# A second early row in every other block of a graph-attention kernel

## The chip, the cores and the metric

The kernel runs on one core of one Trainium2 chip. A core has five engines that each follow their own list of instructions: TensorE (PE in the profile), VectorE (DVE), ScalarE (ACT), GpSimd (POOL) and SyncE (SP), which here only issues DMAs. They meet at semaphores. Sixteen DMA engines move the data. The metric is the device time of one execution, in microseconds.

## The reference

There are N = 30000 nodes with 256 features and E = 510000 edges, sorted by their destination; every edge has one of 8 relations.

```python
x = x + gnn(layernorm(x), conv_weights, attn_l, attn_r, h_bias, src, dst, edge_type)
x = x + ffn(layernorm(x))

def gnn(...):                                   # 8 relations, 4 heads of 64
    feat_all = einsum('ni,rhid->rnhd', inputs, conv_weights)
    feat_src_e, feat_dst_e = feat_all[edge_type, edge_src], feat_all[edge_type, edge_dst]
    el = sum(feat_src_e * attn_l[edge_type], -1)
    er = sum(feat_dst_e * attn_r[edge_type], -1)
    e = leaky_relu(el + er, 0.2)
    alpha = softmax of e over the edges of one destination    # segment max, exp, segment sum
    return segment_sum(alpha * feat_src_e, edge_dst).reshape(N, 256) + h_bias
```

`ffn` is a shared three-layer perceptron plus four experts, each a three-layer perceptron, of which the two with the highest gate are weighed and added.

## The kernel before, in words

The work has two large stages.

**The features.** 235 tiles of 128 nodes are normalised, transposed and multiplied with the weights of all relations and heads (L305). Copies on ACT and DVE (L307, L309) put the products into buffers `fo`, and SyncE stores them (L319) to `feat` in DRAM: one row of 4 x 65 numbers (1040 bytes) for each node and relation, 64 features and the left score of each head. Beside these tiles run three generators, one step at a time in fixed places of the tile loop (`aside`): `edge_records` makes one record of each edge, `places` lays the edges out for attention, and `expert_weights` loads the experts' weights.

`places` cuts the edges into 252 blocks, twelve a batch. Each block has 128 partitions x 16 places (U = 16), each place one edge. It writes a record `rk` for each block to DRAM: the indices of the rows to gather (WI), the destinations (WD), marks (WA), penalties at the borders between destinations (WP), running minima of them (W1) and the one-hot relations (WT).

In each partition one of the 16 edges has the lowest row number. `places` swaps it into place 0 and keeps, in `mark`, where it came from. Because the features are computed in order of the rows, this early row can be fetched before the features end: `first_rows` gathers it on POOL by an indirect DMA into `fr` and SyncE stores four blocks together to `stage` in DRAM. This begins at tile 178 of 235 (`BT + 2`), at a rate of 252 gathers over the tiles that are left, and the gather may touch the first 176 tiles' rows only. A check of the indices leads to a second path of the kernel (`again`) if a row lies beyond.

**Attention.** 252 blocks and one last block of its own form. The loop runs over iterations t, each with six steps c, and the order on every engine is the order in which the code is written (`manual_schedule`). Stages of several blocks are in flight in one iteration:

- `load(t + 2)`: SyncE loads the record `rk` (L903), destinations `dr` (L921), right scores `erp` (L924), residual rows `xt` (L926). `rk` has five buffers.
- `gather(t + 1)`: SyncE loads the early rows from `stage` (L931); POOL issues 15 indirect gathers of one place each (L933) into `ft`, a ring of four blocks. A place of the ring is free when `sums` of the block four earlier is done with it.
- `flags(t + 1)` and `flags_across` spread the penalties (ACT L951 to L955, PE transposes L962, ACT copy L964).
- `dest_select`, `dest_expand` and `dest_pick` (L987 on PE, L998 and L1000 on DVE) give each edge its right score.
- `scores(t)` adds the two scores and takes the running maximum of each destination, forwards and backwards (scans L1032 and L1033, results `fb`). As the swap of `places` has moved one edge of each partition to place 0, `exchange` (L1018, L1020, L1022) swaps the scores to the edges' order before the scans, and `softmax` swaps them again after them.
- `turn_ends` (L1040, L1041), `across` (scans L1047 and L1048), `turn_back` (L1055, L1056) carry the maxima across partitions.
- `softmax` (L1062 to L1065) and `exps` (L1071, L1072) make the weights, `weigh` (L1079) multiplies the rows by them, `onehot` (ACT L1010, L1011) and `sums` (PE L1086) add them by destination into `po`, `finish` divides.
- `residual_sum` adds the input (L1117) and calls `Experts.stats`, the mean and variance for the second layer norm (L722, L723).

Every four blocks one group `Experts` is ready. Its 22 steps (`spread`, `scale` L734, `turn` with the copy L744, the layers L798 to L854, `last` with L857) are taken one in each step c. At the end of a group `last` issues four stores of output rows on SyncE (L1097), in the same queue as the loads.

The parts of `gather` and `exchange` that the change touches read:

```python
nc.sync.dma_start(s.ft[:, 0]..., stage[t * P:(t + 1) * P, :])
for u in range(1 if s.own else 0, s.u):
    nc.gpsimd.indirect_dma_start(out=s.ft[:, u]..., in_=feat[:, :], ...)
```

Of the kernel before, what the change touches and what calls it, by code (L numbers as in the profile page):

```python
# [10 lines left out]
F32 = mybir.dt.float32  # L11
# [10 lines left out]
P = 128  # L22
# [23 lines left out]
WI, WD, WA, WP, W1, WT, WR = 0, U, 2 * U, 3 * U, 4 * U + 1, 6 * U + 3, 6 * U + 3 + U * 4  # L46
# [7 lines left out]
def kernel(  # L54
# [47 lines left out]
    stage = dram.tile([NBLK * P, H * HW], F32, name="stage")  # L102
# [71 lines left out]
    NPEN = 3  # L174
    pens = []
    for i in range(NPEN + 1):
        f = wf.tile([P, H, U if i < NPEN else UL], F32, name=f"penf{i}")
        b = wf.tile([P, H, U if i < NPEN else UL], F32, name=f"penb{i}")
        nc.gpsimd.memset(f, -BIG)
        nc.gpsimd.memset(b, -BIG)  # L180
        pens.append((f, b))
    carry = []
    for i in range(2):
        cf = wf.tile([H, P + 1], F32, name=f"carf{i}")
        cb = wf.tile([H, P + 1], F32, name=f"carb{i}")
        nc.gpsimd.memset(cf, -BIG)
        nc.gpsimd.memset(cb, -BIG)
        carry.append((cf, cb))
# [33 lines left out]
    with ExitStack() as cx:  # L222
# [263 lines left out]
        BT = 3 * NT // 4  # L486
        count = {"ready": 0, "sent": 0}
        low = gp.tile([P, NBLK], I32, name="low")
        lowc = gp.tile([P, NBLK], I32, name="lowc")

        def places(cl):


            GB = 12
# [28 lines left out]
            yield  # L523
            done = None
            for k, (b0, n) in enumerate(batches):
# [4 lines left out]
                key = kp.tile([P, GB, U], F32, name="key", bufs=1)[:, :n]  # L530
                km = kp.tile([P, GB], F32, name="km", bufs=1)[:, :n]
                x = rc[:, :, :U, :3].rearrange("p b u f -> p b f u")
                mark = of[:, :, WA:WA + U]
                nc.vector.scalar_tensor_tensor(key, rc[:, :, :U, 0], float(U),
                                               iu[:, None, :].to_broadcast([P, n, U]), op0=ALU.mult, op1=ALU.add)
                nc.vector.tensor_reduce(km, key, AX.X, ALU.min)
                yield
                if done:
                    done()
                nc.vector.tensor_tensor(mark, key, km[:, :, None].to_broadcast([P, n, U]), op=ALU.is_equal)  # L540
                m3 = mark[:, :, None, :].to_broadcast([P, n, 3, U])
                t3 = kp.tile([P, GB, 3, U], F32, name="t3", bufs=1)[:, :n]
                nc.vector.tensor_mul(t3, x, m3)
                yield
                for f in range(3):
                    nc.vector.copy_predicated(x[:, :, f, 1:], o[:, :, WA + 1:WA + U],
                                              x[:, :, f, 0:1].to_broadcast([P, n, U - 1]))
                yield
                with nc.allow_low_precision(reason="integers below 2 ** 24"):
                    nc.vector.tensor_reduce(x[:, :, :, 0], t3, AX.X, ALU.add)  # L550
                yield
# [3 lines left out]
                nc.gpsimd.tensor_copy(low[:, b0:b0 + n], rc[:, :, 0, 0])  # L555
                nc.gpsimd.tensor_scalar_min(lowc[:, b0:b0 + n], rc[:, :, 0, 0], float(BT * P * R - 1))
                nc.gpsimd.tensor_copy(o[:, :, WI:WI + U], rc[:, :, :U, 0])
                count["ready"] = b0 + n
                pen = kp.tile([P, GB, UW], F32, name="penk")[:, :n]
                nc.vector.tensor_scalar_mul(pen, rc[:, :, :, 3], -BIG)  # L560
                yield
                nc.gpsimd.tensor_copy(of[:, :, WP:WP + UW], pen)
                d16 = kp.tile([P, GB, U], I16, name="d16k")[:, :n]
                nc.gpsimd.tensor_copy(d16, rc[:, :, :U, 1])
                a1 = kp.tile([P, GB, UW], F32, name="a1k")[:, :n]
                a2 = kp.tile([P, GB, UW], F32, name="a2k")[:, :n]
# [7 lines left out]
                nc.gpsimd.tensor_copy(of[:, :, W1 + UW:W1 + 2 * UW], a2)  # L574
                yield
# [7 lines left out]
                def done(o=o, d16=d16, b0=b0, n=n):  # L583
                    nc.sync.dma_start(rk_d[b0:b0 + n].rearrange("b p w -> p b w"), o)
                    nc.sync.dma_start(dk_d[b0 * CAP:(b0 + n) * CAP].rearrange("(b p u) -> p b u", p=P, u=U), d16)
            yield
# [3 lines left out]
            nc.vector.tensor_reduce(exc, low, AX.X, ALU.max)  # L590
# [9 lines left out]
            nc.vector.tensor_scalar(both[:, 0:1], both[:, 0:1], float(BT * P * R), None, op0=ALU.is_ge)  # L600
# [3 lines left out]
        def first_rows():  # L604

            n, kept = 4, []
            fp = cl.enter_context(tc.tile_pool(name="first", bufs=3))

            def keep(b0, m, fr):
                nc.sync.dma_start(stage[b0 * P:(b0 + m) * P, :].rearrange("(b p) f -> p b f", p=P), fr[:, :m])  # L610
            for b0 in range(0, NBLK, n):
                m = min(n, NBLK - b0)
                fr = fp.tile([P, n, H * HW], F32, name="fr")
                for b in range(m):
                    nc.gpsimd.indirect_dma_start(
                        out=fr[:, b], out_offset=None, in_=feat[0:BT * P * R, :],
                        in_offset=bass.IndirectOffsetOnAxis(ap=lowc[:, b0 + b:b0 + b + 1], axis=0))
                    if b == n // 2 and kept:
                        keep(*kept.pop())
                    count["sent"] += 1  # L620
                    yield
                kept.append((b0, m, fr))
            while kept:
                keep(*kept.pop(0))

        with tc.manual_schedule():
# [49 lines left out]
            for m in range(lead, NT - 1):  # L676
                for g in range(NG):
# [6 lines left out]
                    if m >= BT + 2:  # L684
                        fetched = min(fetched + 1.03 * NBLK / ((NT - BT - 2) * NG), 3)
                        while fetched >= 1 and count["sent"] < count["ready"]:
                            next(ahead)
                            fetched -= 1
# [13 lines left out]
    class Experts:  # L702
# [3 lines left out]
        def __init__(self, pool, ph, pc, x1, n, put):  # L706
            self.pool, self.ph, self.pc, self.x1, self.n, self.put = pool, ph, pc, x1, n, put
            self.w = n * M
            self.mv = pool.tile([P, T, 2], F32, name="c_mv", bufs=2)
# [10 lines left out]
        def stats(self, t):  # L720
            st = self.pool.tile([P, 6], F32, name="c_st")
            nc.vector.bn_stats(st[:M], self.x1[:M, t, :])  # L722
            nc.vector.bn_aggr(self.mv[:M, t, :], st[:M])  # L723

        def spread(self):
            self.rs = self.pool.tile([P, T], F32, name="c_rs")
            nc.scalar.activation(self.rs[:M, :self.n], self.mv[:M, :self.n, 1], AF.Sqrt, bias=eps[:M])

        def scale(self, j):
            if j == 0:  # L730
                nc.vector.reciprocal(self.rs[:M, :self.n], self.rs[:M, :self.n])
                self.xn = self.pool.tile([P, T, D], F32, name="c_xn")
            for t in range(j, min(j + 2, self.n)):
                nc.vector.tensor_scalar(self.xn[:M, t, :], self.x1[:M, t, :], self.mv[:M, t, 0:1],  # L734
                                        self.rs[:M, t:t + 1], op0=ALU.subtract, op1=ALU.mult)
# [126 lines left out]
    with ExitStack() as cx:  # L862
# [17 lines left out]
        flat = "p h u -> p (h u)"  # L880
        blk = {}

        class Block:


            def __init__(self, t):
# [7 lines left out]
                self.pens = pens[t % NPEN if t < NBLK else NPEN]  # L894

        def load(t):
# [3 lines left out]
            if s.own:  # L900
# [6 lines left out]
                s.mark, s.marki = rf[:, WA:WA + U], rk[:, WA:WA + U]  # L907
# [497 lines left out]
```

## Time and profile before

| | us |
|---|---|
| runs, median of 3 (lowest to highest) | 8389.48 (8380.45 to 8390.53) |
| profiled execution | 8380.65 |
| its span in the trace | 8379.0 |
| end of the features, about | 1746 |
| first gather of attention | 1750.45 |
| last exponentials, about | 8354 |

The profiled execution is one run. Its span is the time from the first to the last instruction of the trace, and 1.65 us lie around it. Busy time of an engine is the time in which it executes; idle time before an instruction is put down to what released it. "issue" stands for an engine that waited for nothing that the profile shows, and "remote" for a semaphore event whose sender it can't name. A row of the timeline gives start, duration, engine, line, operation, tile names as out<-in, sizes, and in brackets the idle time before it with its releaser. The windows table gives the busy time of each engine in a stretch of time, with the granted clock of PE, the share of the DMA engines that was busy, and the data rate.

### The profile page before, as it was taken

The page shows a single profiled execution, that of the slowest core. Times are in us where ns is not written, and L with a number is a line of the kernel's source. Part 1 is how long each engine was busy: PE and PEld are TensorE (multiplying, and loading weights), DVE is VectorE, ACT ScalarE, POOL GpSimd, SP SyncE. Part 2 cuts the span into 40 slices and gives each one's busy share as a digit, 9 for nine tenths or more (in the row PEclk, how much of TensorE's full clock was granted, in tenths as well). Part 3 has the DMA queues.
Part 4 walks back from the last instruction along what each step waited for, and adds up shares of the span by engine and source line. Part 5 has one row for each costly group of instructions (what it writes and reads, how often), then busy time and mean ns, then how long its engine had stood idle before and what let it go on. Part 6 is the DMA issues. An engine that isn't in the chain of part 4 may idle for free. (4 is left out here: it accounts for less than half of the span.)

```text
span 8379.0 us, 96556 instructions
## 1 busy us (share of the span) xinstructions
PE 6330.2 (76%) x25254; PEld 3986.0 (48%) x25255; DVE 5381.4 (64%) x13882; ACT 3416.7 (41%) x9511; POOL 4073.5 (49%) x4327
## 2 busy tenths in 40 slices
PE   9999999956666767777666667777666777777667
PEld 5555555534444444444444444444444444444444
DVE  5557774447666666666666666666666666666665
ACT  2222222224444444444444444444444444444444
POOL 1101114665555555555555555555555555555552
PEclk9999999978888888888888888888888888888888
DMA  6657778964444444444444444444444444444441
GB/s 226 229 177 238 224 243 303 341 197 123 116 117 117 118 116 119 119 121 119 117 120 117 119 116 118 118 123 118 118 116 117 118 119 118 116 119 117 115 118 55
DMA packets 761457, 1209.52 MB, mean 144 GB/s; under 512 B 241638, under 2 KB 599789, under 8 KB 730685
## 3 DMA queue, kind: packets, MB, share of 16 engines
q1 hardware_dynamic: 565453, 663.56, 24.8%
q0 software_dynamic: 194400, 539.40, 23.3%
q8 instruction: 206, 3.38, 0.2%
q14 instruction: 358, 2.93, 0.1%
q10 hardware_dynamic: 1040, 0.26, 0.0%
HBM read 818.57 MB, written 384.23 MB: 144 GB/s over the span
## 5 line engine op out<-in xcount | busy, mean ns | idle before, releaser
L933 POOL DMA_INDIRECT ft<-feat,rk x3798 | 3608.6, 950 | 2919.9 <-PE po L1086 956.0
L1086 PE MATMUL po<-ft,oh 128*128 128x260 f32 x8100 | 2305.4, 421 | 286.3 <-DVE ho L1107 149.5
L1086 PEld LDWEIGHTS po<-ft,oh 128*128 128x128 f32 x8100 | 1565.4, 208 | 569.7 <-issue 292.4
L305 PE MATMUL ps<-w,xT 128*128 128x448 f32 (+1 forms) x4700 | 1712.6, 519 | 14.3 <-DVE xT L294 8.6
L1079 DVE TENSOR_TENSOR ft<-ft,p 128x768 f32<-128x768 f32 x1518 | 1289.9, 850 | 394.8 <-issue 184.1
L1010 ACT ACTIVATE oh<-icol,rk 128x128 f32<-128x128 f32 x4032 | 1329.1, 389 | 66.4 <-remote 45.5
L305 PEld LDWEIGHTS ps<-w,xT 128*128 128x128 f32 x4700 | 877.3, 191 | 704.9 <-issue 613.5
L798 PE MATMUL ph<-xT,w 128*128 128x512 f32 (+1 forms) x512 | 372.1, 859 | 961.8 <-issue 888.7
L307 ACT COPY fo<-ps 128x448 f32<-128x448 f32 (+1 forms) x711 | 377.3, 533 | 1087.4 <-PE ps L305 912.4
L998 DVE TENSOR_TENSOR ere<-pe,rk 128x384 f32<-128x384 f32 x1008 | 553.3, 549 | 373.4 <-remote 247.9
L1011 ACT ACTIVATE oh<-oh 128x384 f32<-128x384 f32 x1518 | 740.2, 488 | 49.4
L987 PEld LDWEIGHTS <-ohT 128*128 128x128 bf16 x4050 | 393.9, 158 | 548.8 <-issue 438.1
L798 PEld LDWEIGHTS ph<-xT,w 128*128 128x128 f32 x512 | 112.3, 260 | 1112.1 <-issue 952.5
L744 ACT COPY xT<-ph 128x512 f32<-128x512 f32 (+1 forms) x128 | 73.1, 572 | 1325.3 <-remote 1299.9
L1000 DVE TENSOR_REDUCE e<-ere 128x16 f32<-128x384 f32 (+1 forms) x1012 | 561.5, 555 | 34.8
L987 PE MATMUL pe<-erp,ohT 128*128 128x96 bf16 x4050 | 442.3, 236 | 113.3 <-DVE ohT L970 73.5
L798 PE MATMUL ph<-xT,v 128*128 128x512 f32 (+1 forms) x1024 | 500.2, 613 | 2.3 <-ACT h L799 1.5
L1062 DVE TENSOR_TENSOR c<-t,rk 128x128 f32<-128x128 f32 x252 | 71.8, 285 | 618.9 <-remote 582.0
L1071 ACT ACTIVATE p<-e 128x64 f32<-128x64 f32 (+1 forms) x253 | 70.4, 278 | 844.9 <-DVE e L1022 741.8
L307 DVE COPY fo<-ps 128x448 f32<-128x448 f32 (+1 forms) x464 | 242.3, 528 | 221.9 <-PE ps L305 194.2
L1040 PE MATMUL t<-ident,fb 128*4 128x128 f32 x253 | 70.8, 280 | 383.6 <-DVE fb L1033 196.7
L851 PE MATMUL pf<-w,h 128*128 128x256 f32 x506 | 203.2, 491 | 189.1 <-ACT wT L844 85.1
(206 smaller groups left out, 7422.2 us busy)
## 6 DMA issues: line engine op xcount, KB each, us to landing
feat<-fo SPq DMA_DIRECT2D x234, 1040.0 KB
dr<-dk_d SPq DMA_DIRECT2D x252, 516.0 KB
ft<-feat,rk POOLq DMA_INDIRECT x3798
stage<-fr SPq DMA_DIRECT2D x63, 520.0 KB
ft<-stage SPq DMA_DIRECT2D x252, 130.0 KB
xt<-xb_d SPq DMA_DIRECT2D x253, 128.0 KB
out_dram<-og SPq DMA_DIRECT2D x253, 128.0 KB
xb_d<-xb SPq DMA_DIRECT2D x58, 512.0 KB
```

What stands on the lines that cost most here:

```text
L305: nc.tensor.matmul(ps, t["xT"][:, k, :], w[:, k, c0:c1], start=k == 0, stop=k == 1)
L307: eng(t["fo"][:, h0:h1, :HD], ps[:, :n].rearrange("p (a d) -> p a d", d=HD))
L798: nc.tensor.matmul(ps[:, :self.w], lhs, rhs, start=i == 0, stop=i == len(pairs) - 1)
L851: nc.tensor.matmul(pf[:M], self.h2[:, tok], w3, start=True, stop=False)
L933: nc.gpsimd.indirect_dma_start(out=s.ft[:, u].rearrange("p h d -> p (h d)"), out_offset=None, in_=feat[:, :], in_offset=bass.IndirectOffse ...
L987: nc.tensor.matmul(pe[:, u - u0].rearrange("p f r -> p (f r)"), s.ov[:, u, :], s.erp.rearrange("n h k r -> n (h k r)"), start=True, stop=True)
L998: nc.vector.tensor_mul(ere, s.pe[:, :u1 - u0], s.th[:, u0:u1, None, :].to_broadcast([P, u1 - u0, H * 3, R]))
L1000: nc.vector.tensor_reduce(s.e[:, :, u0:u1].rearrange("p h u -> p u h"), ere.rearrange("p u (h k) r -> p u h (k r)", h=H), AX.X, ALU.add)
L1010: nc.scalar.activation(s.oh[:, u, :], icol, AF.Abs, bias=s.nd[:, u:u + 1])
L1011: nc.scalar.activation(s.oh[:, u0:u1], s.oh[:, u0:u1], AF.Relu, bias=1.0, scale=-1.0)
L1079: nc.vector.tensor_mul(fc, fc, pc[:, :, None].to_broadcast([P, (u1 - u0) * H, HD]))
L1086: nc.tensor.matmul(s.po.rearrange("n h d -> n (h d)"), s.oh[:, u, :], s.ft[:, u].rearrange("p h d -> p (h d)"), start=u == 0, stop=u == s. ...
```

## The change

In even blocks the second place holds an early row as well. In the diff, `i` counts the early rows of a block.

- `places` makes a second exchange for every other block, over the places 1 to 15: the lowest row of these goes to place 1. The record holds two marks and grows from 163 to 194 words. A batch takes 11 steps and no longer 9.
- `first_rows` gathers 252 + 126 rows, three to a buffer and store. It starts at tile 156 (`FIRST`), at 1.02 x 378 gathers over the remaining 78 tiles. Each gather may touch the rows stored by then (`rows_there`) and no longer a fixed number of tiles.
- `gather` loads one or two early rows from `stages` and issues 15 or 14 indirect gathers. There are 3672 of them in place of 3798.
- `exchange` is called twice in `scores` and twice in `softmax`; the second call does nothing in odd blocks.
- `flags` makes one copy on ACT in place of four. What `flags_across` computed in each block is made in `places`, twelve blocks at once, written to `thr_d`, and loaded in `load` into `through`.
- `turn_ends` uses two accumulating matmuls, the second against a reversed identity (`turned`), so that both directions run in one scan of eight partitions in `across`, followed by a copy that turns the second half.
- `Experts.stats` and `Experts.scale` move from DVE to ACT: two passes with `accum_out` (Identity and Square) and a small one between them, and the scaling as an activation with scale and bias.

```diff
@@ first_rows, places @@
-        BT = 3 * NT // 4
+        NF = (NBLK, (NBLK + 1) // 2)
+        FIRST = NT * 2 // 3
+        RATE = 1.02 * sum(NF) / (NT - 1 - FIRST)
+        def rows_there(i, b0):
+            at = b0 - b0 % GB if i == 0 else NBLK + b0 - b0 % (GB // 2)
+            return min(NT - 2, int(FIRST + at / RATE) - 2) * P * R
...
+                for i in range(2):
+                    v = rc[:, ::i + 1, i:U]
+                    m, w = (n + i) // (i + 1), U - i
...
+                nc.tensor.transpose(ps[:, :P], a1[:, :, U - 1], ident)
+                nc.tensor.matmul(ps[:, P:], a2[:, :, 1], turned, start=True, stop=True)
+                thr = kp.tile([GB, 2 * P], F32, name="thr")[:n]
+                nc.scalar.copy(thr, ps)
...
-                    if m >= BT + 2:
-                        fetched = min(fetched + 1.03 * NBLK / ((NT - BT - 2) * NG), 3)
+                    if m >= FIRST:
+                        fetched = min(fetched + RATE / NG, 3)
@@ Experts @@
         def stats(self, t):
-            nc.vector.bn_stats(st[:M], self.x1[:M, t, :])
-            nc.vector.bn_aggr(self.mv[:M, t, :], st[:M])
+            nc.scalar.activation(sq[:M], self.x1[:M, t, :], AF.Identity, accum_out=st[:, 0])
+            nc.scalar.activation(st[:, 1], st[:, 0], AF.Identity, scale=-1.0 / D)
+            nc.scalar.activation(sq[:M], self.x1[:M, t, :], AF.Square, bias=st[:, 1], accum_out=st[:, 2])
...
-                nc.vector.tensor_scalar(self.xn[:M, t, :], self.x1[:M, t, :], self.mv[:M, t, 0:1],
-                                        self.rs[:M, t:t + 1], op0=ALU.subtract, op1=ALU.mult)
+                nc.scalar.activation(self.xn[:M, t, :], self.x1[:M, t, :], AF.Identity, bias=rs[:, 1, t:t + 1],
+                                     scale=rs[:, 0, t:t + 1])
@@ load, gather @@
+                self.early = 2 - t % 2 if self.own else 0
...
+                s.through = lp.tile([2 * H, P], F32, name="through", bufs=3)
+                nc.sync.dma_start(s.through, bass.AP(tensor=h.tensor, offset=h.offset, ap=[[P, 2], [0, H], [1, P]]))
...
-                nc.sync.dma_start(s.ft[:, 0].rearrange("p h d -> p (h d)"), stage[t * P:(t + 1) * P, :])
-            for u in range(1 if s.own else 0, s.u):
+            for i in range(s.early):
+                b = t >> i
+                f = b % NS * H * HW
+                nc.sync.dma_start(s.ft[:, i].rearrange("p h d -> p (h d)"), stages[i][b // NS, :, f:f + H * HW])
+            for u in range(s.early, s.u):
@@ flags, exchange, across @@
+            if s.own:
+                nc.scalar.copy(s.pens, s.pen[:, :, None, :].to_broadcast([P, 2, H, n]))
+                return
...
-            exchange(s, s.e)
+            exchange(s, s.e, 1)
+            exchange(s, s.e, 0)
...
-            nc.tensor.transpose(s.t1[:, 0, :], s.f[:, :, s.u - 1], ident)
-            nc.tensor.transpose(s.t1[:, 1, :], s.b[:, :, 0], ident)
+            s.t1 = turned_rows("t1", rows[:, :2 * H, s.u - 1], rows[:, 2 * H:4 * H, 0])
...
-            nc.vector.tensor_tensor_scan(cf[:, 1:], s.through[:, 0, :], s.t1[:, 0, :], -BIG, ALU.add, ALU.max)
-            nc.vector.tensor_tensor_scan(cb[:, P - 1::-1], s.through[:, 1, ::-1], s.t1[:, 1, ::-1], -BIG,
-                                         ALU.add, ALU.max)
+            nc.vector.tensor_tensor_scan(cf[:, 1:], s.through, s.t1, -BIG, ALU.add, ALU.max)
+            nc.vector.tensor_copy(cb, cf[:, P - 1::-1])
```

## The prediction

> **What bounds the kernel now.** I read four views, in this order. The page's busy shares first: no engine is full over the span, so the stages must be taken apart.
>
> ```profile
> PE 6330.2 (76%) x25254; PEld 3986.0 (48%) x25255; DVE 5381.4 (64%) x13882; ACT 3416.7 (41%) x9511; POOL 4073.5 (49%) x4327
> DMA  6657778964444444444444444444444444444441
> ```
>
> The DMA row has its peak (9 and 6) at the end of the features and stands at 4 for the whole attention. So, second, the windows table over the features (columns: window, PE, PEld, DVE, ACT, POOL busy, clock, DMA share, GB/s).
>
> ```profile
> 1200.00:1300.00 100.00, 100.00 (x302) 54.27 (x301) 62.22 (x171) 26.30 (x56) 15.09 (x18) 1.00 0.74 231
> 1400.00:1450.00 50.00, 50.00 (x152) 27.17 (x151) 19.97 (x66) 12.73 (x27) 34.65 (x34) 1.00 1.00 353
> ```
>
> PE is full in both: a tile takes 7.3 us and nothing else shows through. But in the second window, where the early rows are gathered beside the features, the DMA engines are full too, at 353 GB/s. The features have no DMA to spare there.
>
> Third, the waits.
>
> ```profile
> ACT xT L744 <- remote: 1299.9, 63, 22.3
> POOL ft L933 <- PE po L1086: 956.0, 427, 19.8
> DVE c L1062 <- remote: 582.0, 61, 20.3
> ```
>
> 63 times, once for each group of four blocks, ACT waits some 20 us for a PE result in PSUM ("remote": the profile names no sender). The starts of the exponentials (L1071) give the same rhythm: their intervals have medians 36.6, 22.4, 22.0 and 22.2 us, so four blocks take 103.0 us, of which about 14.5 are a stall. Fourth, the timeline across one stall, SyncE's queue and POOL, then who starts again:
>
> ```profile
> 4985.52 13.04 SPq L1097 DMA_DIRECT2D out_dram<-og  x4
> 4999.51 0.33 SPq L903 DMA_DIRECT2D rk<-rk_d  x1
> ...
> 4982.54 0.95 POOL L933 DMA_INDIRECT ft<-feat,rk  x1 [0.30 <-issue]
> 5002.04 0.95 POOL L933 DMA_INDIRECT ft<-feat,rk  x1 [18.55 <-DVE e L1022]
> 5003.30 0.94 POOL L933 DMA_INDIRECT ft<-feat,rk  x1 [0.30 <-issue]
> ...
> 5025.84 0.95 POOL L933 DMA_INDIRECT ft<-feat,rk  x1 [0.30 <-issue]
> 5028.35 0.95 POOL L933 DMA_INDIRECT ft<-feat,rk  x1 [1.56 <-remote]
> ...
> 5033.08 0.58 ACT L744 COPY xT<-ph 128x512 f32<-128x512 f32 x1 [21.43 <-remote]
> 5033.25 0.29 DVE L1062 TENSOR_TENSOR c<-t,rk 128x128 f32<-128x128 f32 x1 [7.79 <-remote]
> ```
>
> The four output rows of a group hold SyncE until 4998.6, so the next record (L903) is late, POOL stands idle for 18.55 us and then runs 20 gathers without a pause, 1.253 us apart. During that run PE falls idle, and ACT and DVE resume together only after it. Over the periods, the restart comes some 31 us after the run's first gather, in steps of about 1.25. How a run of gathers holds PE's results back isn't shown; that the restart follows its end is.
>
> Inside the other three blocks no engine is full (PE 17 to 21, DVE 17 to 18, ACT 9 to 13, POOL 14 of 22 us). They are chains: at the first block after the stall PE waits for the scan.
>
> ```profile
> 5048.78 0.27 PE L1040 MATMUL t<-ident,fb 128*4 128x128 f32 x1 [1.87 <-DVE fb L1033]
> ```
>
> [...]
>
> **The change part by part.** *126 more early rows beside the features.* Attention keeps 3672 of 3798 gathers. The features gain 126 x 133 KB gathered and as much stored, 33.5 MB. The gathers start at tile 156 (about 1157 us) and no longer at 1313. In those 156 us the DMA had 352 - 231 = 121 GB/s free: 18.9 MB. The records' preparation takes 11 and no longer 9 steps a batch, so that some 6 MB of its traffic slide into the same stretch (59 GB/s over 565 to 1266 us is 41 MB; the part after 1157 goes from 16% to 32%). Left over: 33.5 + 6.5 - 18.9 = 21 MB, at 352 GB/s 60 us. The stores' seven output buffers give a few tiles of delay free; I take **+50**, between +10 (all of it finds room) and +90 (POOL late too: 4.94 gathers a tile x 1.253 + 1.5 for casts and records is 7.7 of 7.3 us). PE covers nothing here: when the stores block it, the tile period itself grows.
>
> *The run in the stall.* It is 15 gathers of one block and u = 1 to 5 of the next. The first block is odd (still 15), the next even, whose gathers now start at u = 2. The freed slots end at the same chunk, so the run is one gather shorter: 1.253 x 63 = **-79**. It is 0 if the restart is not tied to the run's end, and -160 if two fall away. SyncE gains a load of `through` each block and one of an early row each second (0.33 to 0.43 each, from L903 and L931's rows), both behind the record that POOL waits for; priced at 0, at most 0.4 x 63 = 25.
>
> *A second exchange in even blocks.* Three DVE instructions twice: 0.226 + 0.232 + 0.221 (L1018, L1020, L1022) and 0.03 gaps, 0.77 each. Two even blocks a period. In the first after the stall the scan is what PE waits for, so the 0.77 in scores is bare: 0.77 x 63 = **+49**. In the third block PE is 1.7 to 3.3 us behind at the low clock, which covers it; the ones in softmax delay the exponentials, where PE has sums queued, and the stall covers the last. Uncovered, each place would cost 49 more; I take 0, at most +98.
>
> *The clock.* The wait at L1040 grows from 1.87 to some 2.6 us[...]. [...] All periods 57, none 0; I take a third: **+19**.
>
> *Flags and turns.* Four ACT copies (0.225 + 0.237 + 0.189 + 0.189) become one of 128 elements[...]; the copy of `through` (0.351) and the two transposes L962 (0.324 each) go. The two L1040/41 transposes become two matmuls of nearly the same size (0.28 each), the second scan (0.382) a copy. DVE -0.18, ACT -0.9, PE -0.65 a block. The wait of ACT for L962 (233.5 us in all) lies in front of onehots that are used one iteration later. **0**, at best -0.3 us in the 190 unstalled blocks, -57.
>
> *Statistics and scaling on ACT.* DVE loses 0.428 + 0.182 + 0.413 a block and gains 0.15 a group twice. [...] ACT is busy for 12.5 of 22, its onehots have an iteration of lead, but it stands in order: the statistics now wait on ACT for the addition (L1117), and behind it the onehots and the experts' copies. Priced **0**; at best DVE's microsecond shows as 0.4 in 190 blocks, -76[...].
>
> Sum: 50 - 79 + 49 + 19 = **+39**. The profiled execution took 8380.65 (span 8379.0 and 1.65 around it), so 8420. That execution is at the low end of the three runs, whose median is 8389.5: the forecast is 0.36% above the median. About 0.2% (17 us) can be told from no change.
>
> **The rivals.** *The relief wins* (faster). One mechanism: DVE, with 17 to 18 of 22 us in a block, is the chain's slow link, and its microsecond and a quarter less a block (bn, scaling, second scan) shortens the three unstalled blocks. For it: ACT's largest named wait in attention is on DVE (L1071 on L1022, 741.8 us). Against it: those instructions lie beside weighing, which waits for nothing. At 0.4 a block (-76), with the run's -79, a bare scan +49 and +10 in the features: 8285. It decides from about 0.25 us a block on: there it outweighs the forecast's +39. If only the features find room and the chain hides the exchange, it is 8310 without any relief.
>
> *The features pay in full*, and the clock falls in every period: +90 + 49 + 57 with -79: 8498. With the run unchanged, 8577. For it: the DMA at 1.00 for 300 us. Against: PE lost only some 8 us there so far.
>
> *The second rows bring nothing*: the restart is tied to something other than the run's end, and the delays hide: +10 to +20 from the features, 8395. For it: restarts scatter in steps. Against: 63 restarts follow a pause of POOL.
>
> **How the numbers follow.** Forecast (slower by 20 to 100) 0.40; features and clock in full 0.12; relief or a well-hidden exchange 0.36; nothing 0.12. The third is below 8373, with about a third of it below 8270, where more than one relief must come together. The forecast's own range is 8405 to 8480. Above 8520 lie table loads and an unchanged run, less than 0.1. So 8270 to 8520; faster 0.36, within 0.2% 0.14, slower 0.50.
>
> **What would show it.** In the windows table from 1160 to 1750: DMA at 1.00 over more than 450 us, PE below full, and the first attention gather later than 1750.45 by about 50. In the timeline over a stall: 19 to 20 gathers and a restart near 30 us after the first. The intervals of the exponentials: 35.4, 23.2, 22.2, 22.2. L1071's table loads stay at 63; more means Square. I am wrong if the unstalled intervals fall below 22.0, if stalls number other than about 63, or if the features end before 1760.

## The result, and the profile after

The changed kernel takes 8479.28 us (median of 4 runs, 8468.05 to 8487.09), the kernel before 8390.01 us. The ratio is 1.0107, with a 95% interval of 1.009 to 1.0125: the change makes the kernel slower by about 89 us. A second pair of the same two kernels (e5 and e6 below) gave 1.0101 (1.007 to 1.0132). The profiled execution after has a span of 8485.4 us, 106.4 more than before. The kernel before took 8390 to 8437 us beside this result and beside e5 to e10, but 6657 to 6659 beside e1 to e4, e11 and e12, whose traces have no stall, so each experiment is compared with the kernel before measured beside it and says "with the stall" or "without".

The page's busy shares and its row of DMA slices:

```profile
PE 6709.1 (79%) x25827; PEld 4201.9 (50%) x25828; DVE 5369.1 (63%) x14119; ACT 3720.1 (44%) x10042; POOL 4104.7 (48%) x4445
DMA  6656678994444444444444444444444444444441
```

PE is busy 379 us longer with only 573 instructions more. The matmuls of the sums, L1086 (now L1156), haven't changed, yet one takes 443 ns in the mean where it took 421: the mean granted clock is 0.862 and no longer 0.877, and from 2200 us on one takes 393 ns (394 after) where the clock record stands at 1.00, and 667 (659) where it stands at 0.50. The DMA row has one slice more at its high end, so the features are longer.

**The stages.** The last feature matmul ends at 1887.3 us and no longer at 1746.2, and the first gather of attention comes at 1907.3 where it came at 1750.45: +157. From there to the end it is 6578.1 us where it was 6628.5: -50. So the features lost three times what attention won. Of the 157, 141 lie before the end of the matmuls. The other 16 follow it: two stores of early rows hold SyncE for 6.51 us (L646 at 1889.99) ahead of the last stores of the features and the first loads of attention.

**The features.** The windows table (window, PE, PEld, DVE, ACT, POOL, clock, DMA share, GB/s), first while `places` still runs beside the early rows, then after it:

```profile
1200.00:1550.00 350.00, 266.11 (x763) 140.11 (x761) 173.33 (x467) 60.98 (x138) 200.28 (x242) 0.88 0.83 274
1600.00:1850.00 250.00, 243.00 (x724) 131.18 (x725) 111.72 (x345) 61.29 (x133) 163.20 (x161) 0.99 0.94 330
```

In the first window PE is idle for 84 of 350 us, and the DMA engines are at 0.83 and 274 GB/s, not at the 353 they reached before. So over this window they are not what is short. The timeline in one of PE's gaps, with other lines left out:

```profile
1237.85 0.95 POOL L653 DMA_INDIRECT fr<-feat,lowc  x1 [13.52 <-DMA stage<-fr]
...
1247.11 2.35 POOL L276 TENSOR_TENSOR xb<-xg,hb 128x1024 f32<-128x1024 f32 x1
...
1249.92 0.56 SPq L253 DMA_DIRECT2D xg<-in_x_dram  x1
...
1256.28 0.43 DVE L142 BATCH_NORM_STATS2 a_st<-xg 128x6 f32<-128x256 f32 x1 [19.12 <-DMA xg<-in_x_dram]
...
1257.96 0.69 PE L294 MATMUL ptr<-ident,a_xn 128*128 128x128 f32 x2 [14.18 <-DVE a_rs L146]
```

POOL stands for 13.52 us because a buffer of early rows isn't stored yet. The addition `xb` (L276) stands behind it on POOL, SyncE's load of the next four tiles of x waits for `xb`, VectorE waits 19.12 us for that load, and PE 14.18 for VectorE. VectorE waits so eight times, 122.0 us in all, and all of PE's 84 us lie between 1240 and 1550. One more gap comes at the end of `places`, where VectorE reads the result of the index check:

```profile
1591.82 0.24 SPq L632 DMA_DIRECT2D exr<-exc_d  x1
...
1598.47 0.27 DVE L635 TENSOR_REDUCE both<-exr 1x1 f32<-1x128 f32 x1 [35.55 <-DMA exr<-exc_d]
...
1601.16 4.99 PE L307 MATMUL ps<-w,xT 128*128 128x448 f32 x8 [31.58 <-DVE xT L296]
```

A few hundred bytes that go to DRAM and back hold VectorE for 35.55 us, as both DMAs stand on SyncE behind early-row stores, and the second waits for the first to land. In the kernel before this wait was 3.6 us.

**Attention.** The waits:

```profile
POOL ft L993 <- DVE m L1090: 905.0, 52, 21.2
ACT xT L790 <- remote: 824.5, 69, 18.5
...
DVE den L1174 <- remote: 277.6, 67, 7.0
```

The wait of ACT for xT fell from 1299.9 to 824.5 us, and one of VectorE for `po` (den) rose: 96.7 us before. With the senders that the trace names counted too, the first falls alike in both pairs, from 1325 to 840 and from 1225 to 843. The second isn't due to the change: in the second trace of the kernel before (e5) it is already

```profile
DVE den L1104 <- remote: 282.2, 67, 7.0
```

as in the changed kernel's second trace (e6, 282.2). Around one stall, first SyncE and POOL, then what follows:

```profile
7783.69 14.99 SPq L1167 DMA_DIRECT2D out_dram<-og  x4
7799.62 0.33 SPq L958 DMA_DIRECT2D rk<-rk_d  x1
...
7802.37 0.95 POOL L993 DMA_INDIRECT ft<-feat,rk  x1 [20.95 <-DVE m L1090]
...
7824.91 0.94 POOL L993 DMA_INDIRECT ft<-feat,rk  x1 [0.30 <-issue]
7829.52 0.94 POOL L993 DMA_INDIRECT ft<-feat,rk  x1 [3.67 <-remote]
```

```profile
7840.96 0.16 DVE L1174 TENSOR_SCALAR den<-po 128x4 f32<-128x4 f32 x1 [3.70 <-remote]
...
7841.94 2.94 PE L1156 MATMUL po<-ft,oh 128*128 128x260 f32 x6 [2.62 <-DVE ho L1177]
...
7844.67 3.35 PE L844 MATMUL ph<-xT,w 128*128 128x512 f32 x4
```

The run is 19 gathers, where its median was 21. The mean intervals of the exponentials go from 36.4, 22.6, 22.0, 22.5 to 32.4, 26.9, 19.9, 23.5 us. The stalled block wins 4.0 and the next loses 4.4, the third wins 2.1 and the fourth loses 1.0. In the period shown a second run of eight gathers follows the first, VectorE gets `po` only in POOL's next pause, PE waits for VectorE, and the four matmuls after that take 3.35 us, where the same four took 1.88 before. In that period the clock of the block is 0.82; in one period before it is 1.00.

Much of this shift isn't the change's either. In e5, the kernel before, the run has a median of 20, a run of eight follows 47 of 61 times (11 of 61 in the first trace before), and the intervals are 34.8, 24.8, 22.5 and 22.3. From e5 to e6 the change takes 2.4 from the stalled block and 3.2 from the third, and adds 2.7 and 1.5 to the two others. What both pairs agree on is that the sum falls a little: the four-block period from 103.6 to 102.7, and from 104.4 to 103.0.

### The profile page after: what moved, and what is told of

Same layout as the page of the kernel before. It is cut to its first block, busy times and chain, and to the rows that moved or that the text cites. A ratio compares the mean times of both kernels' runs of the same rounds, so it can differ in the third digit from the quotient of the medians.

```text
span 8485.4 us, 98942 instructions
## 1 busy us (share of the span) xinstructions
PE 6709.1 (79%) x25827; PEld 4201.9 (50%) x25828; DVE 5369.1 (63%) x14119; ACT 3720.1 (44%) x10042; POOL 4104.7 (48%) x4445
## 3 DMA queue, kind: packets, MB, share of 16 engines
q0 software_dynamic: 194400, 539.40, 22.6%
## 5 line engine op out<-in xcount | busy, mean ns | idle before, releaser
L993 POOL DMA_INDIRECT ft<-feat,rk x3672 | 3484.6, 949 | 2985.1 <-DVE m L1090 905.0
L1156 PE MATMUL po<-ft,oh 128*128 128x260 f32 x8100 | 2458.6, 443 | 481.3 <-DVE ho L1177 258.3
L1156 PEld LDWEIGHTS po<-ft,oh 128*128 128x128 f32 x8100 | 1645.8, 218 | 799.9 <-issue 380.0
L844 PE MATMUL ph<-xT,w 128*128 128x512 f32 (+1 forms) x512 | 424.1, 962 | 456.8 <-issue 389.9
L1070 DVE TENSOR_REDUCE e<-ere 128x16 f32<-128x384 f32 (+1 forms) x1012 | 561.4, 555 | 34.8
L653 POOL DMA_INDIRECT fr<-feat,lowc x378 | 367.7, 973 | 306.7 <-DMA stage<-fr 184.4
L764 ACT ACTIVATE c_sq<-x 128x256 f32<-128x256 f32 x253 | 105.8, 418 | 853.5 <-DVE x L1187 541.7
L1141 ACT ACTIVATE p<-e 128x64 f32<-128x64 f32 (+1 forms) x253 | 70.1, 277 | 914.8 <-DVE e L1093 765.9
L844 PEld LDWEIGHTS ph<-xT,w 128*128 128x128 f32 x512 | 140.2, 304 | 653.8 <-issue 542.9
L790 ACT COPY xT<-ph 128x512 f32<-128x512 f32 (+1 forms) x128 | 73.6, 576 | 840.1 <-remote 824.5
```

The source lines that it names most:

```text
L653: nc.gpsimd.indirect_dma_start(out=fr[:, b], out_offset=None, in_=feat[0:rows_there(i, b0 + b), :], in_offset=bass.IndirectOffsetOnAxis(ap ...
L844: nc.tensor.matmul(ps[:, :self.w], lhs, rhs, start=i == 0, stop=i == len(pairs) - 1)
L993: nc.gpsimd.indirect_dma_start(out=s.ft[:, u].rearrange("p h d -> p (h d)"), out_offset=None, in_=feat[:, :], in_offset=bass.IndirectOffse ...
L1070: nc.vector.tensor_reduce(s.e[:, :, u0:u1].rearrange("p h u -> p u h"), ere.rearrange("p u (h k) r -> p u h (k r)", h=H), AX.X, ALU.add)
L1156: nc.tensor.matmul(s.po.rearrange("n h d -> n (h d)"), s.oh[:, u, :], s.ft[:, u].rearrange("p h d -> p (h d)"), start=u == 0, stop=u == s. ...
```

## The experiments

**e1, the addition off POOL** (without the stall).

```diff
-            nc.gpsimd.tensor_add(xb[:, :n], xg[:, :n], ...)
+            nc.vector.tensor_add(xb[:, :n], xg[:, :n], ...)
```

> The changed kernel, with the addition xb (128x1024, the residual rows) made on VectorE and no longer on GpSimd. Queue theory: in the features GpSimd stands behind early-row gathers that wait for a free buffer, the addition stands behind them, SyncE's next load of x waits for the addition, and PE waits for x. With the addition off GpSimd, PE's gaps of 8 to 32 us between 1240 and 1600 us (119 us in all) mostly go: features end 1760 to 1810 and no longer 1887, total 8370 to 8410. Bandwidth theory (the prediction's step): the 16 DMA engines lack the room, so the features still end within 20 us of 1887 and the total stays at 8460 to 8480.

Measured: 6941.99 us against 6657.22 before, 1.0422 (1.0404 to 1.044). The features end at 1879.0, and PE is idle for 109 us from 1150 on; in e3, whose features are the changed kernel's, it is 1882.8 and 117. So this one way carries almost nothing, and the expected 1760 to 1810 was missed. Waits and SyncE's queue in e1:

```profile
POOL fr L653 <- DMA stage<-fr: 189.4, 42, 23.7
...
DVE a_st L142 <- DMA xg<-in_x_dram: 110.3, 9, 19.6
```

```profile
SPq L646 <- DMA fr<-feat,lowc: 271.5, 79, 10.4
...
1276.75 13.58 SPq L529 DMA_DIRECT2D rcb<-rec  x12
```

x is still late, now because its load stands in SyncE's queue behind stores that wait for gathers to land, and behind twelve loads for `places` that take 13.58 us to issue.

**e2, the second rows gathered in attention again** (without the stall).

```diff
-            for i, n in enumerate(NF):
+            for i, n in enumerate(NF[:1]):
-            for u in range(s.early, s.u):
+            for u in range(min(s.early, 1), s.u):
```

> The changed kernel, but the rows of the second places are gathered in attention again (15 gathers a block, 252 in the features, spread over the same 78 tiles); records, exchanges, flags, scans and statistics stay as changed. If the 126 additional rows cost the features their 141 us, the features end at 1750 to 1790. In attention: if the shorter run of gathers is what shortened the stall, the run is 21 gathers again, the interval of the stalled block goes from 32.1 back to 34.5 to 36.6 us and the four-block period from 102.4 to 104 to 107 us; if the other edits did it, the period stays within 0.5 us. Totals: 8420 to 8560 by the first, 8330 to 8370 by the second.

Measured: 6864.51 us, 1.0306 (1.0285 to 1.0327). The features end at 1797.1, 86 us before those of e3 (1750 to 1790 was expected): the 126 rows cost that much. The other 58 over the kernel before (1739.2 in e12, which has its features) must come from what e2 keeps of the change, the longer `places` and the start at tile 156 beside it. The four-block period is 78.7 us, as in e3 (78.4). Without the stall the gathers saved in attention bring nothing.

**e3, the record one block ahead** (without the stall).

```diff
+                        at(load_rk, t + 3)      # rk alone, ahead of load's other DMAs
                         at(load, t + 2)
```

> The changed kernel, with each record rk loaded one iteration earlier on SyncE (t + 3 in place of t + 2), ahead of the output stores of the group; nothing else moves. Stall theory (SyncE held by the stores starves GpSimd, whose catching-up run then holds PE's results back): GpSimd's idle time of 18 to 21 us before the run goes, no run is longer than some 12, the wait of ACT for xT (824.5 us) falls below 200 us, and the four-block period falls from 102.4 to 88 to 96 us, total 7650 to 8100. Rival (the stall is the experts' chain itself, and the run only coincides with it): the idle time of GpSimd goes, but the period stays at 101 to 103 and the total at 8440 to 8490.

Measured: 6956.21 us, 1.0453 (1.0435 to 1.047), period 78.4. There is no stall that it could remove, so it decides nothing on that. It stands here for the changed kernel without the stall; e1, e3 and e4 have the same period within 0.3 us. So without the stall the change would cost some 4.5%: between the profiled executions of e12 and e3, 160 us up to the first gather of attention and 120 after it.

**e4, rests between the gathers** (without the stall).

```diff
+                if u % 5 == 4:
+                    nc.gpsimd.memset(rest, 0.0)
```

> The changed kernel, with a memset of 128x512 on GpSimd after every fifth place of a block (about 1 us, three a block, priced from the fills of the same engine as an estimate), so that gathers no longer follow each other without a pause. If gathers without a pause are what holds PE's results back, ACT and DVE resume inside the long run and not after it: the wait of ACT for xT falls well below 824 us and the four-block period to 92 to 100 us in spite of 12 us more of GpSimd; total 7850 to 8350. If the length of GpSimd's work matters and not its lack of pauses, the period grows by 3 to 4 us: total 8650 to 8750.

Measured: 6964.02 us, 1.0466 (1.0449 to 1.0484), period 78.3. Nothing is won or lost by the rests, so neither expectation is tested. But the runs without them tell something: in e1 up to 97 gathers follow each other less than 1.3 us apart, in e12 up to 136, and after the first exponentials PE has a single gap over 4.5 us in each. A run of gathers doesn't hold PE's results back everywhere.

**e5 and e6, the two kernels again, with their traces** (with the stall).

> The kernel before, unchanged, for its trace beside those of the other experiments (in the first four runs the kernel before took 6657 us and not 8390). If it again takes about 6657, the stall once in four blocks is absent from its trace: no wait of ACT for xT above 3 us, four-block period 75 to 77 us against the 78.5 of the changed kernel's variants, features ending at 1740 to 1750. If it takes about 8390, the stall is back: 36.6 us in every fourth block and a period near 103.

> The changed kernel, unchanged, as the base of the other runs. Where the kernel before takes about 6657: 6930 to 6960, period 78.3 to 78.7, features ending at 1875 to 1890. Where it takes about 8390: 8470 to 8490, period 102.4, features ending at 1887.

Measured: 8436.44 us (one run) and 8517.9, the latter 1.0101 (1.007 to 1.0132). Features end at 1748.6 and 1893.3, periods are 104.4 and 103.0, intervals 34.8, 24.8, 22.5, 22.3 before and 32.4, 27.5, 19.3, 23.8 after. The split of the result repeats: first gather of attention +157, attention -75.

**e7, the loads of x on ACT's queue** (with the stall).

```diff
-                nc.sync.dma_start(*((d, s) if store else (s, d)))
+                eng.dma_start(*((d, s) if store else (s, d)))       # eng: nc.scalar for x
```

> The changed kernel, with the loads of x (xg) issued from ACT's queue and not from SyncE's. Queue theory, second form: in tiles 156 to 210 SyncE's queue is what is late, since early-row stores wait in it for their gathers to land and twelve loads of rcb take 13.6 us together; the loads of x behind them come up to 20 us late and PE stops. Then 80 to 120 of the 116 to 130 us of PE gaps go, features end 1770 to 1800, and the total is 80 to 110 us below the changed kernel's. Bandwidth theory: features end within 25 us of 1885.

Measured: 8516.06 us, 1.0102 (1.0076 to 1.0128); the features end at 1894.5, and PE is idle for 127 us from 1150 on. x is no longer what VectorE waits for. Its wait has moved to POOL's fill of the new record:

```profile
DVE rko L558 <- POOL rko L541: 73.6, 4, 22.3
```

That fill stands on POOL behind gathers that wait for buffers. My second form of the queue theory fell as the first: one way alone isn't it.

**e8, the statistics on VectorE again** (with the stall).

```diff
+            nc.vector.bn_stats(st[:M], self.x1[:M, t, :])
+            nc.vector.bn_aggr(self.mv[:M, t, :], st[:M])
-            nc.scalar.activation(...)                 # three in stats, one a tile in scale
```

> The changed kernel, with mean, variance and scaling of the second layer norm on VectorE again, as in the kernel before. The features don't change. If the move to ACT costs, since ACT stands still for the addition L1187 (252 waits, 642 us in all) and what is behind it comes late, the four-block period falls by 1 to 3 us (60 to 190 us in all). If the move brings what the prediction's best bound says (0.4 us a block), the period grows by 1 to 1.6 us. The prediction took 0: within 0.3 us.

Measured: 8533.1 us, 1.0122 (1.0096 to 1.0148), period 103.1 as in e6 (103.0). The move of the statistics is worth nothing here, as the prediction had it.

**e9, all ways at once** (with the stall): the twelve loads two a step, fill and addition on VectorE, x on ACT's queue.

```diff
-                for b in range(n):                      # in fetch: all twelve at once
+                pend.extend([lambda b=b: one(b) for b in range(n)])
+            for _ in places_steps(cl):                  # in places: two a step
+                for _ in range(2):
+                    if pend:
+                        pend.pop(0)()
-                nc.gpsimd.memset(o[:, :, WA + U:WA + 2 * U], 0)
+                nc.vector.memset(o[:, :, WA + U:WA + 2 * U], 0)
```

> The changed kernel with four edits in the features alone: the twelve rcb loads of a batch are issued two a step and no longer all at once, the fill of rko and the addition xb are on VectorE and no longer on GpSimd, and the loads of x are issued from ACT's queue. So neither SyncE's queue nor GpSimd's stands between the early rows and the tiles. Coupling theory (each of these ways alone lets another take over, as the run with xb on VectorE and the run with x from ACT showed): while places still runs, the gathers go at 28 or more in 50 us and no longer 22, PE's gaps of 130 us fall below 50, features end 1780 to 1820, total 60 to 110 us below the changed kernel's. Rival (the pipeline of nine fr buffers itself sets the pace, since each must be gathered, landed and stored before it is used again): gathers stay at 20 to 25 in 50 us, and the features end within 25 us of 1890.

Measured: 8474.18 us, 1.0057 (1.0038 to 1.0076): 37 us over the kernel before beside it, where e6 is 88 over its own. The features end at 1849.5, 44 us earlier than in e6. The window, then a wait:

```profile
1200.00:1550.00 350.00, 286.52 (x830) 151.21 (x828) 193.07 (x521) 69.73 (x152) 202.60 (x256) 0.91 0.95 310
...
DVE key L562 <- DMA rcb<-rec: 41.8, 4, 14.7
```

The DMA engines are now at 0.95, nearly full. So the coupling through the queues cost 44 us at least. It isn't all gone: of the remaining 103 us over the kernel before, 41 are one gap, the wait for `exr`, and PE's other gaps after 1250 add up to 40. Most of these follow a wait that e9 makes itself: the `rcb` loads, now spread, come late for VectorE. Gathers go at 24 to 27 in 50 us and not at 28, PE's gaps are 81 us and not below 50, and the features end later than 1820: less than the coupling theory wanted, more than its rival.

**e10, e9 with the record one block ahead** (with the stall; the edits are e9's and e3's).

> As the run before it, and in attention each record rk is loaded one iteration earlier (t + 3), ahead of the group's output stores. On a chip where the kernel before takes about 8400, stall theory (SyncE's stores starve GpSimd, its catching-up run holds PE's results back): GpSimd's idle time of some 20 us before the run goes, no run is over 12, period 88 to 96 us and no longer 102.9, 430 to 940 us less than the run before it. Rival (the results are held back whenever gathers follow each other, wherever their pauses lie): the idle time goes, but the runs become longer, since the gathers are then limited by the ring alone, and the period stays within 3 us. Where the kernel before takes about 6657 there is no stall to remove, and the period stays at 78.5.

Measured: 7718.11 us, 0.9143 (0.9116 to 0.9171) of the kernel before, 756 us below e9, from which it differs in one load's place. The period is 90.9 us (e9: 102.7). After the first blocks POOL is never idle for more than 10 us (e9: 61 times), no run is longer than 11 gathers (e9: 61 of 13 and more), and PE's gaps over 4.5 us after the first exponentials fall from 679 us in all to 313. The waits:

```profile
POOL ft L1010 <- PE po L1173: 883.4, 729, 4.5
...
ACT xT L801 <- remote: 38.9, 7, 7.0
```

POOL now waits briefly and often for free places, and the stall is gone. The rival, in which runs only become longer, is out. This version beats both kernels, where there is a stall. But not all of the difference is gone: e3 has the same code in attention, and its period without the stall is 78.4.

**e11, attention in quarters** (without the stall; one quarter each as changed, with 15 gathers, without the second exchange, with both).

```diff
+            staged = min(s.early, 1) if t // 64 in (1, 3) else s.early
+            if t // 64 < 2:
                 exchange(s, s.e, 1)
```

> The changed kernel with the attention cut in four quarters of 64 blocks, read by their four-block periods; its total is not used. Blocks 0 to 63 are as changed (control, 102.9 where the kernel before takes about 8400). In blocks 64 to 127 the second place's row is gathered in attention again (15 gathers a block). In 128 to 191 the second exchange is left out, so that part of the output is left unordered. In 192 to 251 both. The prediction's steps: 15 gathers lengthen the run by one, +1.25 a period (104.2); without the second exchange -0.8 (102.1); both +0.5 (103.4). Rival (run and period are not tied one to one, since the block after the stall takes back what the stall gives): all four quarters within 0.5 of each other. Where there is no stall (6657): 15 gathers change nothing, and the second exchange is worth up to 3.1 us a period (four calls of 0.77 on the path).

Measured: periods of 78.4, 79.0, 75.6 and 75.6 us. Fifteen gathers for fourteen are within the scatter (e3's own quarters lie from 78.0 to 78.8). The second exchange costs 2.8 us a period, four times some 0.7, so all four places of it lie on the path.

**e12, the kernel before with the record one block ahead** (without the stall; the edit is e3's).

> The kernel before, with each record rk loaded one iteration earlier (t + 3), ahead of the group's output stores, and nothing else. Where the kernel before takes about 8400: the stall goes as it did in the changed kernel, period 88 to 92 us, total 7580 to 7680, so that it beats the kernel before by 9% and the changed kernel with the same edit (7718) by what the features cost that one, 40 to 140 us. If the early rows of the second places are worth something once the stall is gone, its period is longer than 90.9 and the two end within 40 us. Where the kernel before takes about 6657: no change, 6640 to 6670.

Measured: 6659.78 us, 1.0001 (0.9992 to 1.001). The edit is free where there is no stall. Its period is 76.4: without the second exchange the changed kernel (75.6) would be 0.8 below it, with the exchange it is 2.1 above. So the other edits of the change are worth 0.8 us a period and the second exchange takes 2.8. Here GpSimd has hardly a pause left: its gathers start 1.251 us apart in the median, so the 60 of a period take 75.1 of its 76.4 us. The two gathers a period that the change saves could thus bring at most 2.5 us (an estimate, 2 x 1.251), and e11 shows that the rest of the chain doesn't let them: without the second exchange it takes 75.6 us with 58 gathers and with 60. How the kernel before does with this edit where there is a stall wasn't run.

## Why the prediction was right or wrong

**Direction and range: right, in part by luck.** Slower was the likeliest case, 8420 in a range of 8270 to 8520; 8479 was measured, +89 us against +39 over the profile's own time and +30 over the median. But the features missed their own range, and the total stayed inside because attention won 50 us where the terms gave 11.

**126 more early rows, +50 (10 to 90): wrong, +157.** This is the term that was mis-sized. The working counted bytes against the room of the DMA engines. What it had not counted is that the rows now run beside `places`, which ended at 1266 before, ahead of the first gather at 1313, and that both use POOL and SyncE in order. From 1200 to 1550 the gathers go at 20 to 25 in 50 us against 28 to 33 once `places` is done, while the DMA engines have room (0.83). e2, without the stall, splits the loss up to the last matmul: 86 us for the rows themselves, near the top of the range, and 58 for the longer `places` and the early start, which the range didn't hold. e9 shows that at least 44 us are the coupling of the queues. Some 32 to 41 more are one gap of PE at the round trip of the index check; this is read from the traces and wasn't removed by itself. The prediction had POOL's own time a tile (7.7 of 7.3 us), but not what stands behind its gathers: `xb`, the fill, and on SyncE the loads of x and the check. How much of the rest is for want of DMA room isn't separated.

**The shorter run, -79: right in kind, its size uncertain.** The run did become shorter: by two in the first pair (21 to 19) and by one in the second (20 to 19), as forecast. The stalled block won 4.0 and 2.4 us, but over the three blocks after it a good part of that was lost again, so that the period fell by 0.9 and 1.4 us, or 57 and 88 in all. As the kernel before differs that much between its own two traces, the one gather can't be read off a single pair. That attention is tied to what starves POOL is shown by e10, which moves one load and takes 11.8 us from each period. How much of the gain is due to the gathers saved, and how much to the other edits, wasn't separated with the stall; without it they bring nothing (e2, e11).

**The second exchange, +49 with one place of four bare: too small where it could be measured.** Without the stall all four are bare, 2.8 us a period or 176 in all, beyond the bound of 49 + 98. With the stall it wasn't tried.

**The clock, +19: open in attention, and left out in the features.** In the period shown the block after the stall runs at 0.82 and not 1.00, and PE is busy there for 23.5 us and not 19.2. Averaged over 59 periods it has 0.87 where it had 0.93, but in the second pair 0.86 and 0.85, so this one period says too much. In the features the fall is clear in both pairs: from 1150 us on 0.92 and 0.91, where it was 0.99 and 1.00. The working had no term for that. That a longer wait at L1040 brings the clock down, and the 57 us of which +19 is a third, were the author's estimate, and no trace shows it: in e3 PE has no gap over 2.9 us from 2200 us on, and its clock is still 0.95 on average from 2500 to 6000 us, with 104 falls to one half from 2200 us on. In the period shown the clock is at one half from 7840.80 to 7847.62 us; it falls in a gap of 2.62 us in front of the sums, where PE waits for `ho`, and not in the one at L1040. The low clock that the prediction has in the third block was 0.83 before, as a mean over 60 periods.

**Flags, turns, statistics, 0: right for the statistics** (e8, the period within 0.1 us). Table loads, 1.283 us each, stay at 63 at the exponentials (L1141) and 64 at the square root (L770), and none stands at Square (L766). On ACT the six records of statistics and scaling (L764 to L766, L780) take 2.09 us a block, and the one copy of the flags (L1003) 0.282. One reading was wrong: the two accumulating matmuls are not two instructions of 0.28 us but four, 506 at L1024 and 506 at L1025 for 253 blocks, where the transposes L1040 and L1041 were 253 each; the turn back doubles too. So PE's busy time for flags and turns rose by 0.14 us a block (366.9 to 403.2 in all), where the prediction had it fall by 0.65. All edits but the exchange together bring 0.8 us a period without the stall.

**The rivals.** "The features pay in full" came nearest: its +90 was +157, and the clock fell, but in the features for certain only. "The relief wins" held only in that attention became shorter, by 50 to 75 us; its threshold of 0.25 us a block is 0.21 by its own sum (39 over 190). "Nothing" fell.

**The signs.** The run of 19 and the 63 table loads came as named. The first gather came 157 us later and not 50, the intervals were 32.4, 26.9, 19.9 and 23.5 and not 35.4, 23.2, 22.2 and 22.2, and the DMA engines stood at 0.83 and not at 1.00 where PE was below full. The third interval's median is 19.3 us, below the 22.0 under which the prediction called itself wrong: how attention would change, it did not foresee.

**What stays open.** Why PE's results are held back in one set of runs and not in the other, with the same code. Where they are held can be read. In the stall that the prediction shows, the transposes that xT needs end with

```profile
5014.16 0.65 PE L742 MATMUL ph<-ident,c_xn 128*128 128x128 f32 x2 [1.58 <-DVE c_xn L734]
```

and ACT's copy starts at 5033.08, 18 us later. The semaphore records put the delay between the two: PE's updates come in bursts of four and more, less than 0.07 us apart, 261 times in this trace, 221 after and 260 in e10 (from 2200 us on), and never in e3 and e12. The waits of ACT and VectorE over 3 us with no sender named end in a pause of POOL of more than 0.6 us in 136 of 186 cases before and 167 of 218 after, though such pauses make up a third of the time. So late signals and POOL's runs go together; what delays the signals isn't seen in any trace. Why attention won 50 us in one pair and 75 in the other is open too.

## What to carry to other kernels

When work is moved beside other work, check each in-order queue that both use, not only the bandwidth: a load of x that was issued 19 to 24 us ahead of its use before (the five from 1219 us on) comes 19 us too late once stores that wait for gathers stand ahead of it. If a wait goes and the time stays, look at what waits now: here POOL's addition, SyncE's queue and POOL's fill replaced each other, and only all of them together moved the end, with a new wait in their place. When a burst on one engine hurts, look for what starved it just before: the load that came late behind four stores was worth 756 us, over eight times what the change cost. And measure a change more than once before a gap is explained by it: the kernel before had the wait for `po` and the second run of eight by itself in its second trace.

## What the runs showed of the hardware

- With the stall, POOL stood idle for over 10 us 61 times in attention, runs of some 20 indirect gathers followed, and PE's semaphore updates came in bursts (261 in the trace before); the long waits for them ended in a pause of POOL in 136 of 186 cases. Without it (e12) a run of 136 gathers left PE without a gap over 4.5 us, and there was no burst. The load issued earlier, which took 756 us away with the stall (e10), brought nothing without it (e12: 1.0001).
- Indirect gathers followed each other on POOL at 1.251 us in the median (e12), at 1.254 with the stall.
- The float32 matmuls of `turn_ends` were two records of some 0.28 us each (L1024 and L1025: 506 each for 253 blocks), the transposes before were one (L1040: 253, 0.280 us).
- An activation with a sum took 418 + 187 ns (L764: Identity over 256 elements and its READ_ACCUMULATOR) and 510 + 188 ns (L766: Square with a pointer bias); the read is a record of its own.
- Scaling with two pointer operands (L780) took 586 ns for 256 elements.
- A float32 matmul 128x260 of the sums took 393 ns at a clock record of 1.00 and 667 at 0.50 (L1086 in the trace before, from 2200 us on).
- A table load took 1.283 us in all 130 cases of the trace before.
